# Graph attention on neighbour lists: weighing one step later in layer 1, and another staging place for its weight sums

## The chip, the cores and the metric

The kernel runs on one core of one Trainium2 chip, as one program. The metric is the time of an execution in device microseconds (us); where several executions were timed, their median is given. Besides the times there is a profiled execution, whose trace holds each instruction with its engine, its start and its length.

## The reference: what is computed

Two layers of graph attention are computed over N = 2708 tokens of width 512, with 8 heads of 64, in fp32. The adjacency matrix is symmetric, has a one on its diagonal and is otherwise about 0.3% full. Cut to what matters, one layer is:

```python
q = (h @ Wq + bq);  k = h @ Wk + bk;  v = h @ Wv + bv      # 8 heads of 64
scores = q @ k.T / sqrt(64), masked by adj                 # per head
cx = softmax(scores) @ v
h1 = layer_norm(h + cx @ Wo + bo)
out = layer_norm(h1 + relu(h1 @ W1 + b1) @ W2 + b2)        # W1: 512 -> 2048, W2 back
```

## The kernel before: tiles, stages, and what sets the order

**Tokens and neighbours.** The kernel sorts the tokens by their number of neighbours and cuts them into 22 tiles of 128 rows (the last has 20). A table gives each tile its number of neighbour slots, from 22 for the first tile down to 3. A slot is one gather on POOL's queue: 128 rows of keys and values, 128x1024 fp32, 512 KB, fetched from DRAM by a list of indices. A chunk is at most two slots, and lives in one `kv` buffer.

**One chunk of attention.** `weights` (L1154) forms the scores of a chunk on DVE: a product of keys and query (L1156), and a reduction to 8 heads a slot, `sc` (L1162). `weigh` (L1169) lets ACT take the exponentials `p` (L1175) and scale one of the two rows of values (L1182, eight instructions, one for each head), and DVE scale the other (L1188) and add both to a running sum `acc` (L1195). After a tile's last chunk come `sums` (L1199, DVE: L1203 to L1218) and `divided` (L1221, ACT, L1226, eight instructions), which leaves the tile's attention `cx`. The generator `attend` (L1895) makes these calls. In a step it emits the scores of one chunk, then `weigh` for the chunk of the step before, then `sums` for a tile that was weighed in full a step earlier, then `divided`.

**Dense work.** PE transposes `cx` into `cT` (`flip`, L1345: `tp` on PE at L1349, evicted by ACT at L1354), multiplies with Wo (`o`, L626), and runs the feed-forward. The first norm between them is spread over DVE (L1307, L1318, L1334), ACT (squares into `xb`, L1324, and `h<-h,rd`, L1340) and POOL (L1331, L1333). The feed-forward takes two tiles (a block) at a time, through 16 pieces f of 128 hidden columns: `pf` on PE, relu on ACT into `ft` (L1606, or L1778). There are 11 blocks k. From block 2 to block 9 it works by seven products of quarter matrices in place of eight ("by seven", products at L1756), which needs sums of quarters of W2, four for each of seven pairs j of its rows. These sums ("forms") are made on DVE and stored in DRAM, 512 KB a pair; `form_in` and `ask_forms` read them back in layer 1.

**The border of the layers.** While the last block of layer 0 runs, layer 1's matrices are loaded. Its keys and values go to DRAM (`keys_values`), its queries are projected by `query` (PE `q`, DVE `qs` at L1467) and stored (L1478, by SP's or ACT's queue). The transposed input `zT` of a tile is loaded again by SP, by `queries` (L1447, three buffers of tag `cT`, load at L1453) and `two` (L1440, load at L1444).

**Where the forms of layer 1 are staged.** `staged` takes three of the five `kv` buffers (six places of 512 KB), and `form_apart` forms pair j in place j modulo 6 and has ACT's queue store it. Pairs 0 and 1 come at f = 9 and 13 of layer 0's last block, 2 and 3 after its keys, 4, 5 and 6 at layer 1's start. The room of the matrices Wk and Wv (tags `wk` and `wv`, 1 MB each), which layer 1 no longer needs, serves as two more gather buffers from layer 1's first gather on, seven in all.

**Order.** Nothing reorders: each engine runs its instructions in the order in which the code emits them, and a queue issues its DMAs in that order. So an instruction that waits holds up all that stand behind it on its engine. Hand-written tables (`PACE7` and others) say how many steps of `attend` are emitted after each f.

Of the kernel before, what the change touches and what calls it, by code (L numbers as in the profile page):

```python
# [8 lines left out]
F32 = mybir.dt.float32  # L9
# [9 lines left out]
P = 128  # L19
DM = 512  # L20
# [3 lines left out]
NC = DM // P  # L24
# [13 lines left out]
SLOTS = 2  # L38
QB = 3
LAG = 3  # L40
KVB = 5
# [446 lines left out]
def by_edges(ctx: ExitStack, tc: tile.TileContext, x, xT, adj, layers, out, redo):  # L488
# [9 lines left out]
    nc = tc.nc  # L498
# [16 lines left out]
    wts = ctx.enter_context(tc.tile_pool(name="wts", bufs=1))  # L515
# [4 lines left out]
    stage = ctx.enter_context(ExitStack())  # L520
# [15 lines left out]
    at = None  # L536
# [6 lines left out]
    for _ in range(WARM):  # L543
# [16 lines left out]
    form_d = [  # L560
        dram.tile([NFC // 2 - 1, 3 + n, P, 2 * P], F32, name=f"form_d{n}") for n in range(NL)
    ]
# [576 lines left out]
    def chunks_of(g):  # L1139
        S = CAPS[g]  # L1140
        k = (S + SLOTS - 1) // SLOTS
        cuts = [-(-S * i // k) for i in range(k + 1)]
        return [(g, a, b - a) for a, b in zip(cuts, cuts[1:])]
# [87 lines left out]
    places = []  # L1231
    written = [[] for _ in range(NL)]

    def rows_of_keys(n):

        if n == NL - 1 and not places:
            places.extend([None] * KVB + ["wk", "wv"])
        tag = places[0] if places else None
        if places:
            places.append(places.pop(0))  # L1240
        if tag is None:
            return at.tile([P, SLOTS, 2 * DM], F32, tag="kv", name="kv", bufs=KVB)
        kv = wts.tile([P, NC, DM], F32, tag=tag, name="kv")
        return kv.rearrange("p c n -> p (c n)").rearrange("p (s n) -> p s n", s=SLOTS)
# [113 lines left out]
    class Layer:  # L1358
        def __init__(self, n, w):
            self.n, self.w, self.w1, self.w2, self.due = n, w, [], [], None  # L1360
            self.apart, self.other = True, False
            self.stores = nc.sync

# [304 lines left out]

        def staged(self):

            slots = []
            for _ in range(3):
                place = at.tile([P, SLOTS, 2 * DM], F32, tag="kv", name="forms", bufs=KVB)
                place = place.rearrange("p s (i w) -> p (s i) w", w=2 * P)
                slots += [place[:, i : i + 4] for i in (0, 4)]
            return slots

        def form_apart(self, j, slots):

            w, W = self.w2[j], 2 * P  # L1680
            b11, b12, b21, b22 = w[:, 0, :W], w[:, 0, W:], w[:, 1, :W], w[:, 1, W:]
            place = slots[j % len(slots)]
            t2, t3, t4, t1 = (place[:, i] for i in range(4))
            nc.vector.tensor_tensor(t3, b22, b12, ALU.subtract)
            nc.vector.tensor_tensor(t1, b12, b11, ALU.subtract)
            nc.vector.tensor_tensor(t2, b22, t1, ALU.subtract)
            nc.vector.tensor_tensor(t4, b21, t2, ALU.subtract)
            nc.scalar.dma_start(out=form_d[self.n][j].rearrange("i p w -> p i w"), in_=place)

        def form_in(self, j):  # L1690
            W = 2 * P
# [195 lines left out]
    now = Layer(0, layers[0])  # L1887
# [7 lines left out]
    def attend(n, got):  # L1895

        peak = small.tile([P, NT], F32, tag="peak", name="peak", bufs=1)
        nc.vector.memset(peak, 0.0)
        loaded = loads(n)
        steps = []  # L1900
        for g in order:
            cuts = chunks_of(g)
            steps += [(g, s0, c, i, i + 1 == len(cuts)) for i, (_, s0, c) in enumerate(cuts)]
            if g == order[1]:
                steps += [None] * 3
        steps += [None] * 3
        kv = next(loaded)
        yield 0.0
        q, later = asked(n, order[0]), None
        done = [None] * 3  # L1910
        for k, step in enumerate(steps):
            if step:
                g, s0, c, i, last = step
                if i == 0:
                    while q is None:
                        q = asked(n, g)
                        if q is None:
                            yield None
                    t, q = Tile(g, q), None
                if k > 0:  # L1920
                    kv = next(loaded)
                t.weights(kv, s0, c)
                if q is None and g != order[-1]:
                    q, later = later or asked(n, order[order.index(g) + 1]), None
                if g == order[-3] and i == 2:
                    later = asked(n, order[-1])
                done.append((t, kv, s0, c, last))
            else:
                done.append(None)
            t3, t2, t1 = done[-4:-1]  # L1930
            if t1:
                t1[0].weigh(*t1[1:4])
            if t2 and t2[-1]:
                t2[0].sums(peak)
            if t3 and t3[-1]:
                got[t3[0].g] = t3[0].divided()
            yield c / SLOTS if step else 0.2
        nc.vector.tensor_reduce(flags[:, 4 + n : 5 + n], peak, AX.X, ALU.max)
        nc.vector.tensor_scalar(
            flags[:, 4 + n : 5 + n], flags[:, 4 + n : 5 + n], SAFE, None, ALU.is_le  # L1940
        )
# [30 lines left out]

    got = {}
    ahead = attend(0, got)
    early = {}

# [39 lines left out]
    for n in range(NL):  # L2016
        last = n == NL - 1
        nxt = None if last else Layer(n + 1, layers[n + 1])
        if n > 0:
            streamed = now.queries(order[10:16])  # L2020
            got = {}
            ahead = attend(n, got)
            for j in (4, 5):
                now.query(*pool.pop(0))
                now.form_apart(j, staged)
            next(ahead)
            both = now.two(order[8:10])
            pool += [(g, both[:, i]) for i, g in enumerate(order[8:10])]
            next(streamed)
            now.stores = nc.scalar  # L2030
            now.form_apart(6, staged)
            while pool:
                if len(pool) < 5:
                    advance(0.65)
                now.query(*pool.pop(0))
            for i, _ in enumerate(streamed):
                if i == 1:
                    both = now.two(order[16:18])
                if i == 4:
                    now.stores = nc.sync  # L2040
                if len(got) < 2 or i < 3:
                    advance(0.65)
            until(blocks[0][0])
            early[n] = now.attended(blocks[0], got, None, True)
            next(early[n])
            now.query(order[16], both[:, 0])
            until(blocks[0][1])
            next(early[n])
            for _ in blocks[0]:
                next(early[n])  # L2050
            streamed = now.queries(order[18 : 2 * AHEAD])
            next(streamed)
            now.query(order[17], both[:, 1])
            advance(0.6)
            next(streamed)
            advance(0.6)
            *_, hs = early[n]
            early[n] = hs, now.turned(blocks[0], hs)
            asking = now.queries(blocks[AHEAD])
            next(asking)  # L2060
            finish(streamed)
            now.apart = False
            now.load_w2(NFC // 2 - 1)
        hs, hT = early[n]
        projecting = xbs = tail = None
        for k, block in enumerate(blocks):
# [14 lines left out]
            for f, zs in enumerate(working):  # L2081
# [31 lines left out]
                    now.load_w2(len(now.w2), nc.scalar)  # L2113
                if n > 0 and (k, f) == (0, 2):
                    now.load_second(1, temp)
                if n == 0 and k == FORMED[0] and f in FORMS:
                    now.form(FORMS.index(f))
                if n > 0 and k == FORMED[n] and f > 4 and f % 2:
# [27 lines left out]
                if not last and not more:  # L2146
                    if f % 2:
                        nxt.load_w1(f // 2)
                        if f > 2:
                            nxt.load_w2(f // 2 - 1)  # L2150
                    if f == 6:
                        nxt.load_first()
                        nxt.load_second(0, temp)
                        staged = nxt.staged()
                    if f in (9, 13):
                        nxt.form_apart(f // 4 - 2, staged)
                    if f == 13:
                        nxt.settle()
                    if f == 7:
                        finish(ahead)  # L2160
                        pool += nxt.preloaded(order[:8], temp)
# [5 lines left out]
        if not last:  # L2167
            nxt.wq = now.wq
            for _ in range(2):
                nxt.query(*pool.pop(0))  # L2170
                if len(pool) % 2:
                    next(behind)
            nxt.kept()
            for g in order[:2]:
                own[g] = asked(n + 1, g)
            finish(behind)
            behind = None
            for j in (2, 3):
                nxt.form_apart(j, staged)
            now = nxt  # L2180
    return again

# [54 lines left out]
```

## Time and profile before

| | |
|---|---|
| median of 3 runs | 1836.91 us (1832.55, 1836.91, 1836.97) |
| profiled execution | 1836.3 us, its span in the trace 1834.3 us |
| mean granted clock of PE in it | 0.994 |
| last keys of layer 0 issued to DRAM (POOL L1082) | 1075.03 us into the span |

PE is TensorE's matmuls, DVE is VectorE, ACT ScalarE, POOL GpSimd, SP SyncE; SPq, ACTq and so on are the sequencers that issue DMAs. In a row of the timeline, start and length come first, then engine, line, operation, output<-inputs and the number of instructions drawn together; in brackets stands the idle time ahead of it and what ended that. Among the DMA queues q0 carries POOL's transfers, q1 and q10 those of SP and ACT.

### The profile page before, as it was taken

The numbers are of one execution on the slowest core, as the hardware profiler recorded it, in microseconds if no ns is written. First come the engines' busy times: TensorE is split into PE (matmuls) and PEld (weight loads), VectorE is DVE, ScalarE is ACT, GpSimd is POOL, SyncE is SP. The second block draws the span as 40 slices with busy tenths as digits, with TensorE's granted clock in tenths as the row PEclk, the third lists the DMA queues.
The fourth block names the chain that finished last, engine by engine and source line by source line (L and its number), as shares of the span: only waits on it lengthen the run. The fifth ranks groups of instructions, "written<-read, shape, count | busy, mean of one in ns | idle before, by whom it ended". The sixth has DMA issues, their size and how long they took to land.

```text
span 1834.3 us, 24263 instructions
## 1 busy us (share of the span) xinstructions
PE 1794.1 (98%) x6931; PEld 1234.3 (67%) x6931; DVE 1483.3 (81%) x2667; ACT 1002.9 (55%) x3399; POOL 860.5 (47%) x827
## 2 busy tenths in 40 slices
PE   9999999999999999999999999999999999999997
PEld 4444456666777867778677543665787788788775
DVE  4987778988989889899885276988989988989952
ACT  4771435645556545564553112677666767667641
POOL 3333755534455544454430022645655655665512
PEclk9999999999999999999999999999999999999999
DMA  9997987756576675665652886957968776786721
GB/s 339 370 335 246 372 281 248 233 171 234 197 253 227 199 235 196 218 237 182 225 185 80 277 305 244 335 155 268 307 201 281 237 252 218 278 262 189 241 81 32
DMA packets 193928, 432.25 MB, mean 236 GB/s; under 512 B 21222, under 2 KB 91482, under 8 KB 193784
## 3 DMA queue, kind: packets, MB, share of 16 engines
q0 software_dynamic: 76560, 262.92, 42.9%
q1 hardware_dynamic: 103370, 142.42, 23.0%
q10 hardware_dynamic: 13854, 25.28, 3.7%
q8 instruction: 57, 0.93, 0.2%
q14 instruction: 87, 0.71, 0.1%
HBM read 362.63 MB, written 57.11 MB: 229 GB/s over the span
## 4 chain that ended last, share of the span: by engine, by line
PE 76%; DVE 12%; issue 5%; ACT 4%; DMA 2%; POOL 1%; DVEq 0%; POOLq 0%; ACTq 0%
PE pf L1767 18%; PE c L1756 8%; PE q L626 7%; PE k L626 7%; PE v L626 7%; PE o L626 7%; PE a L1756 6%; PE pf L1595 5%; PE a L1568 4%; DVE sc L1162 2%; DVE kv L1156 2%; PE tp L1349 2%; PE a L1787 1%; PE a L1791 1%; ACT kv L1182 1%
## 5 line engine op out<-in xcount | busy, mean ns | idle before, releaser
L1119 POOL DMA_INDIRECT kv<-kv_d,listed x420 | 538.2, 1282 | 295.0 <-DVE acc L1195 131.7
L1767 PE MATMUL pf<-hT,w 128*128 128x256 f32 x2048 | 465.6, 379 | 3.3 <-ACT ft L1778 3.3
L1767 PEld LDWEIGHTS pf<-hT,w 128*128 128x128 f32 x2048 | 387.4, 190 | 68.5 <-issue 12.0
L1182 ACT ACTIVATE kv<-kv,p 128x64 f32<-128x64 f32 x1232 | 311.0, 335 | 5.0
L1156 DVE TENSOR_TENSOR kv<-kv,q 128x1024 f32<-128x1024 f32 (+1 forms) x222 | 257.2, 1159 | 16.1 <-DMA q<-q_d,ident_i 10.9
L1162 DVE TENSOR_REDUCE sc<-kv 128x16 f32<-128x1024 f32 (+1 forms) x222 | 258.0, 1162 | 7.6
L1195 DVE TENSOR_TENSOR acc<-acc,kv 128x1024 f32<-128x1024 f32 (+2 forms) x178 | 205.6, 1155 | 51.6 <-ACT kv L1182 36.4
L1778 ACT ACTIVATE ft<-pf,b 128x256 f32<-128x256 f32 x192 | 88.8, 466 | 227.4 <-PE pf L1767 220.3
L1175 ACT ACTIVATE p<-sc,listed 128x8 f32<-128x8 f32 x420 | 103.5, 294 | 124.3 <-DVE sc L1162 96.0
L1281 POOL TENSOR_TENSOR rd<-va,mhalf 128x1 f32<-128x1 f32 (+1 forms) x48 | 43.8, 913 | 253.0 <-DVE va L1279 252.5
L626 PE MATMUL o<-wo,cT 128*128 128x512 f32 x336 | 152.8, 599 | 5.0 <-ACT ft L1606 3.6
L1595 PEld LDWEIGHTS pf<-hT,w 128*128 128x128 f32 x768 | 130.2, 190 | 39.5 <-issue 25.5
L1595 PE MATMUL pf<-hT,w 128*128 128x256 f32 (+1 forms) x768 | 155.1, 350 | 0.1
L1568 PE MATMUL a<-w,ft 128*128 128x512 f32 x288 | 135.1, 592 | 0.0
L1188 DVE TENSOR_TENSOR kv<-kv,p 128x512 f32<-128x512 f32 (+1 forms) x178 | 124.0, 697 | 5.9 <-ACT p L1175 5.7
L626 PEld LDWEIGHTS o<-wo,cT 128*128 128x128 f32 x336 | 64.0, 192 | 73.9 <-issue 61.1
L1331 POOL TENSOR_SCALAR va<-sq 128x1 f32<-128x1 f32 (+1 forms) x40 | 16.9, 424 | 200.3 <-ACT xb L1324 95.8
L751 DVE MAX8 tops<-code 128x8 f32<-128x247 f32 (+2 forms) x242 | 79.1, 400 | 29.3 <-ACT code L746 29.3
L1226 ACT ACTIVATE cx<-acc,su 128x64 f32<-128x64 f32 (+1 forms) x352 | 88.2, 333 | 11.1 <-DVE su L1218 8.6
L1182 ACT ACTIVATE acc<-kv,p 128x64 f32<-128x64 f32 (+1 forms) x352 | 88.9, 335 | 1.4
L746 ACT ACTIVATE code<-aj 128x1354 bf16<-128x1354 int32 (+1 forms) x44 | 74.0, 1724 | 25.9 <-POOL aj L740 21.8
L1756 PE MATMUL c<-w,forms 128*128 128x256 f32 x288 | 85.7, 379 | 0.0
(257 smaller groups left out, 2880.5 us busy)
## 6 DMA issues: line engine op xcount, KB each, us to landing
forms<-form_d SPq DMA_DIRECT2D x336, 128.0 KB
aj<-in_adj SPq DMA_DIRECT2D x42, 677.0 KB
kv_d<-kvs ACTq DMA_DIRECT2D x21, 512.0 KB
h<-ln_b POOLq DMA_DIRECT2D x41, 256.0 KB
xg<-in_xT SPq DMA_DIRECT2D x19, 512.0 KB
w<-in_W SPq DMA_DIRECT2D x16, 512.0 KB
kv<-kv_d,listed POOLq DMA_INDIRECT x420
zT_d<-zT SPq DMA_DIRECT2D x22, 256.0 KB
```

Of the source, the lines that this page charges most:

```text
L626: nc.tensor.matmul(o[:r], xs(c), wm[:, c, :], start=(c == 0), stop=(c == NC - 1))
L1119: return nc.gpsimd.indirect_dma_start(out=to, out_offset=None, in_=table[:, :], in_offset=bass.IndirectOffsetOnAxis(ap=s, axis=0), bounds_ ...
L1156: nc.vector.tensor_tensor(kv[:r, :c, :DM], kv[:r, :c, :DM], self.q[:r].unsqueeze(1).to_broadcast([r, c, DM]), ALU.mult,)
L1162: nc.vector.tensor_reduce(self.sc[:r, s0 : s0 + c, :], kv[:r, :c, :DM].rearrange("p s (h d) -> p s h d", d=DK), AX.X, ALU.add,)
L1175: nc.scalar.activation(p[:r, s, :], self.sc[:r, s, :], AF.Exp, bias=minus[:r, g, s : s + 1])
L1182: nc.scalar.activation(to[:, i, hd], kv[:r, i, DM + h * DK : DM + (h + 1) * DK], AF.Copy, scale=p[:r, s0 + i, h : h + 1],)
L1188: nc.vector.tensor_tensor(to[:, 0, :].rearrange("p (h d) -> p h d", d=DK), kv[:r, 0, DM:].rearrange("p (h d) -> p h d", d=DK), p[:r, s0, : ...
L1195: nc.vector.tensor_tensor(self.acc[:r, :c, :], self.acc[:r, :c, :], kv[:r, :c, DM:], ALU.add)
L1568: nc.tensor.matmul(a[:r, cols], fts[f][:, c0 : c0 + r], self.w2[f // 2][:, f % 2, cols], start=(f == 0), stop=(f == NFC - 1),)
L1595: nc.tensor.matmul(pf[:, :w], self.w1[f // 2][:, c, f % 2 * P : f % 2 * P + P], hT[:, c, :w], start=(c == 0), stop=(c == NC - 1),)
L1756: nc.tensor.matmul(to, left, right, start=start, stop=stop)
L1767: nc.tensor.matmul(pf[:, :W], self.w1[j][:, c, f % 2 * P : f % 2 * P + P], hT[:, c, :], start=(c == 0), stop=(c == NC - 1),)
```

## The change

The change has three parts.

1. In layer 1 `weigh` stands two steps behind the scores in place of one (`late = 1 + n`). `sums` and `divided` of a tile come at the start of the step after, ahead of that step's scores. Four empty steps in place of three let the tail run out. Layer 0 keeps its order.
2. The forms of layer 1 are staged elsewhere. Pairs 0, 1 and 2 are formed in two `kv` buffers in layer 0's last block (f = 9, 12, 15) and stored by POOL's queue. Pairs 3 and 4 are formed in the room of Wk after the last keys, pairs 5 and 6 in the room of Wv at layer 1's start.
3. These last four pairs are stored only in layer 1's first block, at f = 3 to 6, by SP's queue. The rooms of Wk and Wv become gather buffers behind that, at f = 7; until then gathers have five buffers.

```diff
     def rows_of_keys(n):
         if n == NL - 1 and not places:
-            places.extend([None] * KVB + ["wk", "wv"])
+            places.extend([None] * KVB)
...
         def staged(self):
-            slots = []
-            for _ in range(3):
-                place = at.tile([P, SLOTS, 2 * DM], F32, tag="kv", name="forms", bufs=KVB)
-                place = place.rearrange("p s (i w) -> p (s i) w", w=2 * P)
-                slots += [place[:, i : i + 4] for i in (0, 4)]
-            return slots
+            if not self.stages:
+                for _ in range(2):
+                    self.stages.append(
+                        at.tile([P, SLOTS, 2 * DM], F32, tag="kv", name="forms", bufs=KVB)
+                    )
+                return
+            for i, tag in enumerate(("wk", "wv")):
+                place = wts.tile([P, NC, DM], F32, tag=tag, name="forms")
+                self.stages.append(place.rearrange("p (s a) n -> p s (a n)", s=SLOTS))
+        def stage(self, j):
+            place = self.stages[j // 2 if j < 3 else (j + 1) // 2]
+            place = place.rearrange("p s (i w) -> p (s i) w", w=2 * P)
+            a = 4 * (j % 2 if j < 3 else (j + 1) % 2)
+            return place[:, a : a + 4]
-        def form_apart(self, j, slots):
+        def form_apart(self, j):
...
-            place = slots[j % len(slots)]
+            place = self.stage(j)
...
-            nc.scalar.dma_start(out=form_d[self.n][j].rearrange("i p w -> p i w"), in_=place)
+        def form_out(self, j, by):
+            to = form_d[self.n][j].rearrange("i p w -> p i w")
+            by.dma_start(out=to, in_=self.stage(j))
...
     def attend(n, got):
-        steps = []
+        steps, late = [], 1 + n
...
-                steps += [None] * 3
-        steps += [None] * 3
+                steps += [None] * (late + 2)
+        steps += [None] * (late + 2)
...
-        done = [None] * 3
+        done = [None] * 5
+        def ends():
+            t3, t2 = done[-3 - late], done[-2 - late]
+            if t2 and t2[-1]:
+                t2[0].sums(peak)
+            if t3 and t3[-1]:
+                got[t3[0].g] = t3[0].divided()
         for k, step in enumerate(steps):
+            if late > 1:
+                done.append(None)
+                ends()
+                done.pop()
...
-            t3, t2, t1 = done[-4:-1]
+            t1 = done[-1 - late]
             if t1:
                 t1[0].weigh(*t1[1:4])
-            if t2 and t2[-1]:
-                t2[0].sums(peak)
-            if t3 and t3[-1]:
-                got[t3[0].g] = t3[0].divided()
+            if late == 1:
+                ends()
...
-            for j in (4, 5):
+            for j in (5, 6):
                 now.query(*pool.pop(0))
-                now.form_apart(j, staged)
+                now.form_apart(j)
...
-            now.form_apart(6, staged)
...
+                if n > 0 and k == 0 and 2 < f < 7:
+                    now.form_out(f, nc.sync)
+                if n > 0 and (k, f) == (0, 7):
+                    places.extend(["wk", "wv"])
...
-                        staged = nxt.staged()
-                    if f in (9, 13):
-                        nxt.form_apart(f // 4 - 2, staged)
+                        nxt.staged()
+                    if f in (9, 12, 15):
+                        nxt.form_apart(f // 3 - 3)
+                        nxt.form_out(f // 3 - 3, nc.gpsimd)
...
-            for j in (2, 3):
-                nxt.form_apart(j, staged)
+            nxt.staged()
+            for j in (3, 4):
+                nxt.form_apart(j)
```

PE's order of instructions is the same in both kernels. The other engines' orders differ at many places; three follow.

ACT at the border, before: `kvs<-v` are the last values of layer 0, `form_d` the stores of forms, `q_d<-qs` the stores of queries, and `p` and `acc` the first weighing of layer 1.

```order
L1873 COPY kvs<-v 20x512
L1873 COPY kvs<-v 128x512
L1688 DMA form_d_118<-forms 128x4x256 x5
L1478 DMA q_d_114<-qs 128x512 x2
L1175 ACTIVATE p<-sc,listed 128x8 x2
L1182 ACTIVATE acc<-kv,p 128x64 x8
```

The same place on ACT in the changed kernel:

```order
L1886 COPY kvs<-v 20x512
L1886 COPY kvs<-v 128x512
L1479 DMA q_d_114<-qs 128x512 x3
L1175 ACTIVATE p<-sc,listed 128x8 x2
L1182 ACTIVATE acc<-kv,p 128x64 x8
```

The five stores of forms are gone from ACT's queue. POOL, at the same border in the changed kernel, has three of the seven stores, ahead of the last keys (`kv_d`) and the first gathers (`kv<-kv_d`):

```order
L1082 DMA kv_d_112<-kvs,ident_i 2708x1024 x2
L1701 DMA form_d_118<-forms 128x4x256 x3
L1281 TENSOR_TENSOR rd<-va,mhalf 20x1
L1281 TENSOR_TENSOR rd<-va,mhalf 128x1
L1869 MEMSET zT 128x512
L1082 DMA kv_d_112<-kvs,ident_i 2708x1024 x2
L1119 DMA kv<-kv_d_112,listed 128x1024 x18
```

The other four stand on SP's queue in layer 1's first block, among loads of layer-norm rows (`ln_b`) and of queries (`q<-q_d`):

```order
L581 DMA ln_b<-in_ln_b 128x512
L1701 DMA form_d_118<-forms 128x4x256 x2
L1116 DMA q<-q_d_114 128x512
L1701 DMA form_d_118<-forms 128x4x256 x2
L1479 DMA q_d_114<-qs 20x512
```

ACT at the end of block 4 of layer 1 (f = 12 to 15), before; the squares `xb,sq` and `h<-h,rd` are steps of the norm ahead of block 5, and `hT` evicts its transposes:

```order
L1324 ACTIVATE xb,sq<-h,nm 128x512
L1778 ACTIVATE ft<-pf,b_8175 128x256
L1175 ACTIVATE p<-sc,listed 128x8 x2
L1182 ACTIVATE kv<-kv,p 128x64 x8
L1226 ACTIVATE cx<-acc,su 128x64 x8
L1778 ACTIVATE ft<-pf,b_8175 128x256
L1340 ACTIVATE h<-h,rd 128x512 x2
L1778 ACTIVATE ft<-pf,b_8175 128x256
L1354 ACTIVATE hT<-tp,ln_b 128x128 x8
```

And in the changed kernel:

```order
L1324 ACTIVATE xb,sq<-h,nm 128x512
L1791 ACTIVATE ft<-pf,b_8175 128x256
L1175 ACTIVATE p<-sc,listed 128x8 x2
L1182 ACTIVATE acc<-kv,p 128x64 x8
L1791 ACTIVATE ft<-pf,b_8175 128x256
L1340 ACTIVATE h<-h,rd 128x512 x2
L1791 ACTIVATE ft<-pf,b_8175 128x256
L1354 ACTIVATE hT<-tp,ln_b 128x128 x8
L1226 ACTIVATE cx<-acc,su 128x64 x8
```

The eight `cx` moved from ahead of `h<-h,rd` to behind `hT`. At the end of block 3 eight `cx` stand ahead of `h<-h,rd` in both kernels.

DVE in the last block by seven (k = 9), before: a step's weighing is the pair L1188 and L1195, the sums for the seven products are L1733 to L1736, and L1203 begins the `sums` of the last tile:

```order
L1162 TENSOR_REDUCE sc<-kv 128x16
L1188 TENSOR_TENSOR kv<-kv,p 128x512
L1195 TENSOR_TENSOR acc<-acc,kv 128x1024
L1733 TENSOR_TENSOR forms<-ft 128x128
L1734 TENSOR_TENSOR ft<-ft 128x128
L1735 TENSOR_TENSOR forms<-forms,ft 128x128
L1736 TENSOR_TENSOR forms<-ft,forms 128x128
L1188 TENSOR_TENSOR kv<-kv,p 128x512
L1195 TENSOR_TENSOR acc<-acc,kv 128x1024
L1203 TENSOR_TENSOR acc<-acc 128x512
```

And in the changed kernel, from the same sums on:

```order
L1749 TENSOR_TENSOR forms<-ft,forms 128x128
L1188 TENSOR_TENSOR kv<-kv,p 128x512
L1195 TENSOR_TENSOR acc<-acc,kv 128x1024
L1188 TENSOR_TENSOR kv<-kv,p 128x512
L1195 TENSOR_TENSOR acc<-acc,kv 128x1024
L1746 TENSOR_TENSOR forms<-ft 128x128
L1747 TENSOR_TENSOR ft<-ft 128x128
L1748 TENSOR_TENSOR forms<-forms,ft 128x128
L1749 TENSOR_TENSOR forms<-ft,forms 128x128
L1203 TENSOR_TENSOR acc<-acc 128x512
```

One more weighing and one more set of sums for the products now stand between the last scores and the last tile's `sums`.

More of the change, by code (lines that the diff above doesn't have):

```diff
@@ L1360, in __init__ @@
             self.n, self.w, self.w1, self.w2, self.due = n, w, [], [], None
+            self.stages = []
             self.apart, self.other = True, False
```

## The prediction, made before the changed kernel ran

> **What bounds it now.** First the page: the busy times and their shares of the span.
>
> ```profile
> PE 1794.1 (98%) x6931; PEld 1234.3 (67%) x6931; DVE 1483.3 (81%) x2667; ACT 1002.9 (55%) x3399; POOL 860.5 (47%) x827
> ```
>
> PE is the bound, and the change leaves its instructions and their order alone. So a gain can come only from PE's idle time and from stretches at a lower clock. Second, PE's waits (us in total, times, longest):
>
> ```profile
> PE q L626 <- DMA zT<-zT_d: 4.5, 2, 3.6
> PE tp L1349 <- ACT h L1340: 4.2, 3, 2.4
> PE o L626 <- ACT ft L1606: 3.6, 1, 3.6
> PE pf L1767 <- ACT ft L1778: 3.3, 5, 1.1
> ```
>
> All four lie at the border or in layer 1 in the main. Third, the timeline of PE at the three large ones, and at two small ones:
>
> ```profile
> 1101.43 13.90 PE L626 MATMUL q<-wq,zT 128*128 128x512 f32 x32
> 1116.15 3.67 PE L626 MATMUL q<-wq,zT 128*128 128x512 f32 x8 [0.82 <-DMA zT<-zT_d]
> 1123.46 6.70 PE L626 MATMUL q<-wq,zT 128*128 128x512 f32 x8 [3.64 <-DMA zT<-zT_d]
> 1130.00 0.60 PE L1349 MATMUL tp<-ident,cx 128*128 128x128 f32 x4
> ...
> 1261.72 5.40 PE L626 MATMUL o<-wo,cT 128*128 128x512 f32 x8 [3.60 <-ACT ft L1606]
> 1401.74 1.99 PE L1767 MATMUL pf<-hT,w 128*128 128x256 f32 x8 [1.07 <-ACT ft L1778]
> 1466.99 1.73 PE L1349 MATMUL tp<-ident,h 128*128 128x128 f32 x8 [2.41 <-ACT h L1340]
> 1593.03 1.27 PE L1349 MATMUL tp<-ident,h 128*128 128x128 f32 x8 [1.41 <-ACT h L1340]
> ```
>
> Eight matmuls of q take 13.90 / 4 = 3.47 us, but 6.70 after the wait at the border, and eight of o 5.40. The windows say why; the third number from the end of a row, ahead of DMA share and GB/s, is the granted clock:
>
> ```profile
> 1125.00:1127.00 2.00, 2.00 (x3) 0.67 (x2) 1.93 (x6) 0.19 (x1) 0.00 (x0) 0.50 0.00 0
> 1260.00:1270.00 10.00, 8.28 (x23) 4.52 (x24) 9.43 (x15) 8.59 (x34) 2.02 (x2) 0.83 0.76 299
> 1465.00:1475.00 10.00, 8.01 (x29) 6.13 (x30) 7.92 (x12) 9.73 (x37) 7.72 (x7) 0.83 0.91 284
> ```
>
> After a long wait the clock stands at 0.50 for a while. A mean of 0.83 over 10 us is 3.4 us at half speed, some 1.7 us of work lost on top of the wait. So the three places cost: border, 1101.43 to 1130.00 is 28.6 us for six tiles worth 20.8, so 7.8 (4.5 of it waits); 1261, 3.6 + 1.7 = 5.3; 1467, 2.4 + 1.7 = 4.1. With the smaller waits (4.2 - 2.4 and 3.3, so 5.1 at most), all that the change can touch is about 22 us.
>
> By the Trainium skill (TensorE: Matmul & The Clock Gate, What's actually happening) the clock has two values, half and full, and falls after an idle window of about 3.4 us. The halves agree. The wait of 2.41 us at 1467 was followed by 3.4 us of half clock too, so here the measurement decides; counted by the page's figure, that place would be worth 2.4 in place of 4.1.
>
> **The border: stores taken away.** The late loads are the fifth and sixth zT. The DMA engines are the cause:
>
> ```profile
> DMA packets 5603, 10.56 MB, mean 341 GB/s; under 512 B 402, under 2 KB 2962, under 8 KB 5602
> ...
> q0 software_dynamic: 424, 1.54, 67.9%
> q10 hardware_dynamic: 212, 0.40, 17.3%
> q1 hardware_dynamic: 213, 0.39, 16.8%
> ```
>
> The first row is 1074 to 1105, the queues are 1110 to 1116 (packets, MB, share): the engines are full, mostly with POOL's gathers (q0). The issues around it:
>
> ```profile
> 1074.22 11.08 ACTq L1688 DMA_DIRECT2D form_d<-forms  x5
> ...
> 1095.72 0.99 POOL L1119 DMA_INDIRECT kv<-kv_d,listed  x1 [7.37 <-DVE kv L1156]
> ...
> 1105.06 3.75 SPq L1453 DMA_DIRECT2D zT<-zT_d  x2
> 1111.92 0.32 SPq L1453 DMA_DIRECT2D zT<-zT_d  x1
> ```
>
> The sixth zT, asked at 1111.92, is read at 1123.46, 11.5 us for 256 KB. To be in time it would have to be there at 1116.15 - 0.82 + 3.47 = 1118.8, 4.7 us sooner. Removed from these 31 us are the five stores, 5 x 0.52 = 2.6 MB: 7.7 us of DMA at 341 GB/s. Two of them freed the `kv` buffers that held POOL up to 1095.72; after that it issued twelve gathers back to back, 6.3 MB, into the window in which the zT were asked. With five gather buffers in place of seven, 2 MB of these come later still. Against that, three stores (1.6 MB) move to POOL's queue ahead of the last keys: formed at f = 9 to 15, some 20 us sooner, so two are gone before; only the third (1.5 us at 341) may push the keys. I take it as hidden by the projections that run on PE then. Net 2.6 MB + up to 2 MB less, 7.7 to 13 us against the 4.7 needed: both zT in time. PE then runs on to the transpose of block 0's second `cx`:
>
> ```profile
> 1126.81 0.35 ACT L1226 ACTIVATE cx<-acc,su 128x64 f32<-128x64 f32 x1 [2.57 <-DVE su L1218]
> ```
>
> This `cx` was ready at 1128.8, and PE would want it near 1125.7 with nothing lost. It comes sooner with no gather late, and later by the step that `weigh` stands back, for which DVE has room (it waits 1.54 us for a gather at 1103, quoted below). Estimate: 1 us of wait remains. Bounds: nothing to 7.8 gained; I take -7.0.
>
> **Weighing two steps back.** At 1261 PE waits for `ft`, and ACT was held up ahead of it, by scores just made:
>
> ```profile
> 1258.52 0.49 ACT L1175 ACTIVATE p<-sc,listed 128x8 f32<-128x8 f32 x2 [1.41 <-DVE sc L1162]
> ...
> 1260.96 0.45 ACT L1606 ACTIVATE ft<-pf,b 128x256 f32<-128x256 f32 x1
> ...
> 1251.69 1.22 DVE L1156 TENSOR_TENSOR kv<-kv,q 128x1024 f32<-128x1024 f32 x1
> 1256.01 1.22 DVE L1156 TENSOR_TENSOR kv<-kv,q 128x1024 f32<-128x1024 f32 x1
> ```
>
> A chunk is 4.32 us of DVE. Two steps back, `p` asks for scores 4.3 us older, so the wait of 1.41 and the lateness behind it go: -5.3 (bounds 0 and -5.3). What DVE waits for ACT goes the same way:
>
> ```profile
> DVE acc L1195 <- ACT kv L1182: 15.7, 18, 1.6
> 1127.00:1757.00 630.00, 620.08 (x2565) 472.02 (x2563) 558.62 (x902) 428.16 (x1545) 356.55 (x323) 0.99 0.74 242
> ```
>
> (Waits, then the window, both of layer 1: DVE is busy 558.6 of 630 us, 89%.) But DVE is the next bound. PE comes 12 us sooner to blocks 2 and 3 and DVE has its chunks still to do, so part comes back: at block 3's end eight `cx` (2.0 us of ACT) still stand ahead of `h<-h,rd`, where PE lost 1.07 at 1401. I take +1 in block 2 and +2.5 in block 3, between nothing and the whole 5.3.
>
> At 1467 the reason is on ACT in plain sight:
>
> ```profile
> 1463.97 2.00 ACT L1226 ACTIVATE cx<-acc,su 128x64 f32<-128x64 f32 x8
> 1466.23 1.32 ACT L1340 ACTIVATE h<-h,rd 128x512 f32<-128x512 f32 x2
> ```
>
> Without these eight `cx` (they move behind `hT`), `h<-h,rd` comes 2.0 sooner; of the wait of 2.41 0.4 to 0.5 remains and the half clock goes: -3.4. For the other small waits I take -1.5 of 5.
>
> The last block pays. There the last tile's `cx` is what PE waits for next:
>
> ```profile
> 1752.26 0.28 DVE L1733 TENSOR_TENSOR forms<-ft 128x128 f32<-128x128 f32 x1
> 1753.39 0.68 DVE L1188 TENSOR_TENSOR kv<-kv,p 128x512 f32<-128x512 f32 x1
> 1755.44 0.69 DVE L1203 TENSOR_TENSOR acc<-acc 128x512 f32<-128x512 f32 x1
> ...
> 1757.03 2.02 ACT L1226 ACTIVATE cx<-acc,su 128x64 f32<-128x64 f32 x8 [0.98 <-DVE su L1218]
> 1758.05 1.38 PE L1349 MATMUL tp<-ident,cx 128*128 128x128 f32 x4
> ```
>
> One set of sums (1752.26 to 1753.39, 1.1) and one weighing (2.0) come ahead of L1203 in addition, and the transposes follow `cx` at once: +3.0, less where DVE is ahead by then (bounds 0 and 3.1, and with half clock behind it 4.8).
>
> The four stores on SP in layer 1's first block cost nothing by themselves: 2.1 MB, 6 us of DMA that the gathers share, while PE there never stopped.
>
> ```profile
> 1150.00:1160.00 10.00, 10.00 (x40) 7.41 (x39) 8.32 (x11) 8.15 (x33) 8.48 (x8) 1.00 1.01 387
> ```
>
> Their cover is DVE's slack there, 17%. SP's loads of queries stand behind them, asked a tile ahead.
>
> Sum: -7.0 - 5.3 + 3.5 - 3.4 - 1.5 + 3.0 = -10.7, from 1836.3 to 1825.6. That execution is 0.6 under the median of 1836.9, so 1826.
>
> **Rivals.** *All of it goes:* DVE's 15.7 us of waits give it the room, nothing comes back and the last block pays nothing: -7.8 - 5.3 - 4.1 - 4 = -21, 1815.5. For it: 11% of DVE idle. Against: the order in the last block. Chance 0.15.
>
> *The zT stay late:* between 1110 and 1116 three queues share, 68 : 17 : 17, so that SP's queue gets its 17% share as long as POOL's has gathers, whatever was stored before. Then 256 KB still take about as long as now, the border gives 1 to 3 in place of 7: 1831 to 1833. The Trainium skill has this (DMA: Bandwidth & Descriptors, Queues, rings and completion order): each engine takes turns among the queues, a packet each; the 424, 212 and 213 packets agree in so far as the two hardware queues have equal counts. Against: the backlog behind the sharing is what shrinks. Chance 0.12.
>
> *DVE takes it back:* what layer 1 gains in one block it waits for in the next, as DVE is 89% busy; only the border's 7 less the last block's 3 remain: 1832.5. Chance 0.09.
>
> *Slower, five buffers starve DVE:* at the border a gather released at 1095.72 was read at
>
> ```profile
> 1103.84 1.23 DVE L1156 TENSOR_TENSOR kv<-kv,q 128x1024 f32<-128x1024 f32 x1 [1.54 <-DMA kv<-kv_d,listed]
> ```
>
> 8.1 us later. With five buffers, each now held a step longer, the cover is two chunks, 2 x 4.32 = 8.6. It decides from 8.6 on: with the stores of forms in the same stretch a landing of 10.5 would cost 1.9 for each of some 14 chunks, 27 us of DVE against 17% slack over 80 us, 14; the rest, 13, shows on PE in blocks 0 and 1, less the border's 7 and 3 more: 1840. Chance 0.10.
>
> **Numbers.** The forecast has 0.54, its own range 1821 to 1831. Low 1816 leaves out half of the first rival, high 1838 most of the last: together under 2 in 10. A measurement of this kernel tells 0.3%, 5.5 us: faster is forecast and first rival, 0.69 + 0.01; same is the two at 1832 to 1833, 0.21; slower the last, most of it, 0.09.
>
> **What would show it.** Right: in PE's waits the row q <- zT is gone, no 0.50 at 1125; no o <- ft; no 2.4 of tp <- h, a wait of tp for `cx` near 1755 instead. DVE's wait for L1182 well under 15.7. Wrong: DVE kv <- DMA rows between 1130 and 1210; POOL gathers that wait for L1188 or L1195 there; tp <- h or pf <- ft rows of the old sum at other blocks.

## The result: slower by 0.56%, and the profile after

The changed kernel takes 1844.61 us in the median of 7 runs (1841.11 to 1847.77), the kernel before 1833.24 of 7 (1831.03 to 1836.97). The ratio is 1.0056, with a 95% interval of 1.0041 to 1.0072: slower by about 11 us, outside the forecast range and on the other side of zero. The profiled execution took 1847.77 us (span 1845.7).

PE's busy time and its waits, from the page and the view of waits of the changed kernel (us in total, times, longest):

```profile
PE 1800.1 (98%) x6931; PEld 1238.0 (67%) x6931; DVE 1484.4 (80%) x2667; ACT 1000.9 (54%) x3399; POOL 844.1 (46%) x830
```

```profile
PE pf L1780 <- ACT ft L1791: 8.7, 5, 4.2
PE o L626 <- ACT cT L1354: 7.6, 4, 5.2
PE tp L1349 <- ACT h L1340: 4.0, 3, 2.3
...
PE tp L1349 <- ACT cx L1226: 2.6, 2, 2.5
```

The row of q waiting for zT is gone (4.5 before), and so is o waiting for ft (3.6). In their place stand waits for `cT`, for `ft` in the blocks by seven, and for `cx`. The timeline of PE shows where. (The two o of a block are multiplied inside the feed-forward of the block before it: those of block 1 begin at 1196, inside block 0, and those of block 2 at 1263 and 1272, inside block 1.)

```profile
1105.28 20.80 PE L626 MATMUL q<-wq,zT 128*128 128x512 f32 x48
...
1196.39 6.28 PE L626 MATMUL o<-wo,cT 128*128 128x512 f32 x7 [5.17 <-ACT cT L1354]
...
1263.21 3.60 PE L626 MATMUL o<-wo,cT 128*128 128x512 f32 x8
1272.30 3.27 PE L626 MATMUL o<-wo,cT 128*128 128x512 f32 x7 [1.61 <-ACT cT L1354]
...
1409.55 1.27 PE L1349 MATMUL tp<-ident,h 128*128 128x128 f32 x8 [2.28 <-ACT h L1340]
...
1721.78 2.50 PE L1780 MATMUL pf<-hT,w 128*128 128x256 f32 x5 [4.17 <-ACT ft L1791]
...
1769.37 1.91 PE L1349 MATMUL tp<-ident,cx 128*128 128x128 f32 x4 [2.48 <-ACT cx L1226]
```

The first row is the border: all six tiles of queries run through in 20.8 us, without a wait. At the first o of block 1 the kernel before had

```profile
1194.14 3.70 PE L626 MATMUL o<-wo,cT 128*128 128x512 f32 x8 [0.40 <-ACT cT L1354]
```

PE's instructions stand in one order in both kernels, so the start of each can be set against its like. Over the border the changed kernel gains 6.6 us against the kernel before, and at the first o of block 2 (1263) another 5.6. It loses 7.8 at the first o of block 1 (1196, a wait of 5.17 where 0.40 was, and half clock), 1.9 at 1272, 6.3 in blocks 2 and 3, 4.6 in block 8 (1721) and 5.4 in the last block by seven (1769), and gains 3.7 from block 4 to block 7. From the border to PE's last matmul layer 1 is 16.7 us longer; behind that, while the last rows go out, it gains 2.7. (Ahead of layer 0's last block, where the two kernels have the same order, the changed one's execution is already 3.8 us behind. That is a spread between executions: the kernel below with cheaper empty steps has the changed kernel's order up to the border as well, and its execution comes there 5.6 us sooner.)

DVE's waits in layer 1, in the changed kernel:

```profile
DVE acc L1195 <- ACT kv L1182: 22.9, 23, 1.6
DVE kv L1188 <- ACT p L1175: 9.1, 9, 2.0
...
DVE kv L1156 <- DMA kv<-kv_d,listed: 3.3, 2, 2.2
```

DVE waits more for ACT than before (L1195 15.7, L1188 2.5), though its scores are a chunk older. It waits little for gathers, 3.3 us in all, but 2.24 of them stand ahead of the wait at 1196:

```profile
1165.17 1.23 DVE L1156 TENSOR_TENSOR kv<-kv,q 128x1024 f32<-128x1024 f32 x1 [2.24 <-DMA kv<-kv_d,listed]
```

### The profile page after: what moved, and what is told of

It reads as the page before. It is cut to its first block, busy times and chain, and to the rows that moved or that the text cites. A ratio compares the mean times of both kernels' runs of the same rounds, so it can differ in the third digit from the quotient of the medians.

```text
span 1845.7 us, 24269 instructions
## 1 busy us (share of the span) xinstructions
PE 1800.1 (98%) x6931; PEld 1238.0 (67%) x6931; DVE 1484.4 (80%) x2667; ACT 1000.9 (54%) x3399; POOL 844.1 (46%) x830
## 5 line engine op out<-in xcount | busy, mean ns | idle before, releaser
L1119 POOL DMA_INDIRECT kv<-kv_d,listed x420 | 524.2, 1248 | 370.5 <-DVE acc L1195 174.6
L1195 DVE TENSOR_TENSOR acc<-acc,kv 128x1024 f32<-128x1024 f32 (+2 forms) x178 | 205.6, 1155 | 60.1 <-ACT kv L1182 43.4
L1188 DVE TENSOR_TENSOR kv<-kv,p 128x512 f32<-128x512 f32 (+1 forms) x178 | 123.7, 695 | 13.7 <-ACT p L1175 12.3
L1769 PE MATMUL a<-w,forms 128*128 128x256 f32 x288 | 85.7, 379 | 0.0
```

The lines of the kernel that those rows point to most:

```text
L1119: return nc.gpsimd.indirect_dma_start(out=to, out_offset=None, in_=table[:, :], in_offset=bass.IndirectOffsetOnAxis(ap=s, axis=0), bounds_ ...
L1188: nc.vector.tensor_tensor(to[:, 0, :].rearrange("p (h d) -> p h d", d=DK), kv[:r, 0, DM:].rearrange("p (h d) -> p h d", d=DK), p[:r, s0, : ...
L1195: nc.vector.tensor_tensor(self.acc[:r, :c, :], self.acc[:r, :c, :], kv[:r, :c, DM:], ALU.add)
L1769: nc.tensor.matmul(to, left, right, start=start, stop=stop)
```

## The experiments

The kernels were timed in three sets, each beside the kernel before (the third set on another chip). The median of the latter moved between 1831.5 and 1835.4 from set to set, so ratios are given against the runs of the same set.

**First set: the parts apart.** The staging alone, weighing one step behind:

```diff
-        steps, late = [], 1 + n
+        steps, late = [], 1
```

> The staging of the forms as in the change, weighing one step behind in layer 1 as before. Theory 1 (the loss lies in the weighing two steps behind; the staging is good): the border keeps its gain of 6.6 us, the wait of 3.6 us for ft at block 1 and the 2.4 us at block 4 stay; 1826 to 1829 against 1833 before, PE's wait o <- cT at block 1 under 1 us or back by part of the gain. Theory 2 (five buffers and stores moved into block 0 cost more than they bring): 1836 to 1842, with DVE waits for gathers (kv <- DMA) over 10 us in layer 1.

Measured: 1826.64 us against 1835.4, ratio 0.9953 (0.9941 to 0.9966). PE's waits of this kernel from the border on:

```profile
PE tp L1349 <- ACT h L1340: 3.9, 3, 2.1
PE o L626 <- ACT ft L1607: 3.6, 1, 3.6
PE q L626 <- DMA zT<-zT_d: 2.3, 2, 1.3
...
PE o L626 <- ACT cT L1354: 0.3, 1, 0.3
```

Layer 1 is as before, the border is cheaper (2.3 of waits for zT without half clock behind them, not nothing), and behind the border DVE waits for no gather. Theory 2 falls.

The weighing two steps behind alone, with the staging as before (the loop of `attend` from the changed kernel, its four empty steps with it, in the kernel before):

> Weighing two steps behind with the sums and cx at the next step's start, the forms staged as before. Theory 1: the border still costs its 7.8 us, and layer 1 loses: PE comes to block 0 6.6 us later, so that the new wait of 5.2 us for cT there is nearly gone, the others (ft 4.2 us in block 8, cx 2.5 us in the last block, half clock behind them) stay: 1839 to 1845. DVE's waits for ACT (L1195 and L1188) at 25 us or more, as in the change (32), against 18 before. Theory 2: 1826 to 1830, since only the lag's gains are left.

Measured: 1844.99 us, 1.0059 (1.0046 to 1.0072). Theory 1's upper end: without the better border it is as slow as the whole change, and its waits in block 8 (4.2) and for the last `cx` (2.8) are those of the changed kernel. The wait at the first o of block 1, expected to be nearly gone with PE later there, is 3.0:

```profile
1195.99 3.70 PE L626 MATMUL o<-wo,cT 128*128 128x512 f32 x8 [3.00 <-ACT cT L1354]
```

DVE's two waits for ACT were 32.4 us. For gathers, with seven buffers, it did not wait behind the border.

The whole change, with `cx` at the end of a step in place of the next one's start:

```diff
-            if late > 1:
-                done.append(None)
-                ends()
-                done.pop()
+            if late > 1:
+                add_up(1)                 # sums of the tile weighed in the step before
...
-            if late == 1:
-                ends()
+            if late == 1:
+                add_up(0)
+            divide(late - 1)              # cx of the tile whose sums this step made
```

> The change, with the division cx taken from the next step's start to the end of the step in which the sums are made (behind that step's weighing, and ahead of the dense work that is emitted between two steps). Theory 1 in the form that cx comes too late on ACT, behind ft that wait for PE: PE's waits for cx and cT (10.2 us in layer 1) fall by half or more, 1836 to 1841. If DVE's pace alone sets layer 1: no change, 1843 to 1846.

Measured: 1838.35 us, 1.0015 (1.0006 to 1.0025). So some 6 us (1844.6 to 1838.4) come back by the place of `cx` in the order alone. But PE's waits for `cT` and `cx` fell only from 10.2 to 9.4 us; those for `ft` fell, from 7.1 to 3.7 with the 1.3 that the view gives to issue. The time was as expected, the place was not.

The whole change with three empty steps behind the first block's tiles:

```diff
             if g == order[1]:
-                steps += [None] * (late + 2)
+                steps += [None] * 3
```

> The change, with three empty steps in place of four behind the first block's tiles, as before. If the extra empty step is what makes the scores of block 1's tiles fall behind a query that PE makes late (DVE waited 3.6 us for q at 1149 there): PE's wait for cT at 1196 (5.2 us and 3.4 at half clock) falls to 2 or less, 1837 to 1840. If DVE was late for other reasons: 1843 to 1846.

Measured: 1831.21 us (1828.49 to 1836.15), 0.998 (0.9969 to 0.9991), below both readings. One empty step, which adds no instruction, is worth 13.4 us in the medians; in the profiled executions 10.9 of it lie between the border's first query and PE's last matmul. But again not where expected: the wait for `cT` at block 1 stayed, and those in block 8 and for the last `cx` were gone.

```profile
PE o L626 <- ACT cT L1354: 6.4, 2, 4.7
PE tp L1349 <- ACT h L1340: 5.4, 4, 1.4
PE q L626 <- DMA zT<-zT_d: 2.6, 1, 2.6
PE pf L1780 <- ACT ft L1791: 0.8, 1, 0.8
```

**Second set: why an empty step costs.** `attend` is paid by the piece: after each f its steps are emitted while a budget lasts, a chunk of two slots costs 1 and an empty step 0.2. One empty step more puts later steps 0.2 later against PE's pieces. (Steps that are emitted because PE's next work needs a tile's `cx` are not paid, so that equal prices in sum need not give an equal order.)

```diff
-            yield c / SLOTS if step else 0.2
+            yield c / SLOTS if step else 0.6 / (late + 2)
```

> The change with its four empty steps, each paid at 0.15 of a step in place of 0.2, so that the four cost the order's budget what three did. If the loss of 13 us between four and three empty steps comes from the budget (all later steps of attention are emitted 0.2 of a step later against PE's pieces f): 1830 to 1834. If it comes from the empty step itself (block 0's second tile ends a step later): 1841 to 1846.

Measured: 1835.05 us (1829.32 to 1841.44), 1.0002 (0.9987 to 1.0016). 9.6 of the 13.4 us come back; the median lies a little above the range that was expected, and the runs lie 12 us apart. So the price of empty steps alone, without an instruction more or less, moves the time by some 10 us. But the order that it gives is not that of three steps, and PE's waits are others:

```profile
PE pf L1780 <- ACT ft L1791: 6.6, 3, 4.4
PE o L626 <- ACT cT L1354: 3.8, 2, 2.8
...
PE tp L1349 <- ACT cx L1226: 1.5, 1, 1.5
```

The wait in block 8 (4.4) is there, as with four steps at the full price; the gain lies between the first o of block 1 and block 4. That the shift by 0.2 makes the difference between three and four steps, place for place, is thus not shown.

The same empty step without the lag (in the staging alone, four in place of three, and this in both layers):

> Staging alone (weighing one step behind), with four empty steps at 0.2 in place of three. If the place of the steps against the pieces f is what costs, with or without the lag: 1833 to 1842 against 1826.6 with three. If an empty step more hurts only together with the lag: 1825 to 1829.

Measured: 1833.84 us, 0.9992 (0.9981 to 1.0002), so 7.2 us more than the staging alone, whose ratio was 0.9953 (0.9941 to 0.9966). Not all of it is layer 1's. The edit lengthens layer 0's order too, and of the 8.1 us between the two profiled executions 4.4 lie ahead of the border, 2.7 of them as waits that the staging alone doesn't have:

```profile
276.92 1.99 PE L1596 MATMUL pf<-hT,w 128*128 128x256 f32 x8 [1.75 <-ACT ft L1607]
292.32 1.99 PE L1596 MATMUL pf<-hT,w 128*128 128x256 f32 x8 [0.93 <-ACT ft L1607]
```

From the border on the fourth step costs 3.7 us, between the two readings. In layer 1 the two orders differ at few places, and the trace shows one chain whole. DVE with three empty steps, and then with four:

```profile
1141.38 0.69 DVE L1468 SCALAR_TENSOR_TENSOR qs<-q,bq 128x512 f32<-128x512 f32 x1 [0.36 <-PE q L626]
1141.99 1.22 DVE L1156 TENSOR_TENSOR kv<-kv,q 128x1024 f32<-128x1024 f32 x1
...
1145.69 0.69 DVE L1468 SCALAR_TENSOR_TENSOR qs<-q,bq 128x512 f32<-128x512 f32 x1 [0.64 <-PE q L626]
```

```profile
1144.89 0.69 DVE L1468 SCALAR_TENSOR_TENSOR qs<-q,bq 128x512 f32<-128x512 f32 x1 [0.36 <-PE q L626]
1149.20 0.69 DVE L1468 SCALAR_TENSOR_TENSOR qs<-q,bq 128x512 f32<-128x512 f32 x1 [3.62 <-PE q L626]
1149.81 1.22 DVE L1156 TENSOR_TENSOR kv<-kv,q 128x1024 f32<-128x1024 f32 x1
```

With three, a chunk's scores stand between two `qs`; with four, the second `qs` has come ahead of them, and DVE waits for PE to finish that query, 3.62 us, with the scores behind it. 44 us later PE, which has not waited since, finds the first o of block 1 short of its `cT`; the first row is with three empty steps, the second with four:

```profile
1187.19 3.70 PE L626 MATMUL o<-wo,cT 128*128 128x512 f32 x8 [0.32 <-ACT cT L1354]
```

```profile
1193.54 4.97 PE L626 MATMUL o<-wo,cT 128*128 128x512 f32 x7 [3.15 <-ACT cT L1354]
```

The changed kernel has the same pair of `qs`, with the same 3.62 us:

```profile
1145.57 0.69 DVE L1468 SCALAR_TENSOR_TENSOR qs<-q,bq 128x512 f32<-128x512 f32 x1 [0.36 <-PE q L626]
1149.88 0.69 DVE L1468 SCALAR_TENSOR_TENSOR qs<-q,bq 128x512 f32<-128x512 f32 x1 [3.62 <-PE q L626]
```

On ACT the lateness arrives as a wait for DVE's sums `su`, and the eviction `cT`, whose transposes PE had finished at 1187.8, stands behind it:

```profile
1188.48 2.02 ACT L1226 ACTIVATE cx<-acc,su 128x64 f32<-128x64 f32 x8 [4.06 <-DVE su L1218]
...
1195.98 1.11 ACT L1354 ACTIVATE cT<-tp,bv 128x128 f32<-128x128 f32 x4
```

But the lag with three empty steps has the pair too (3.62, at 1150.70), and so its wait at block 1 stayed. From the second `qs` to the first o of block 1 it takes 44.3 us with the fourth step and no lag, and 44.2 with the lag and the staging as before, but 46.5 in the changed kernel, whose DVE waits 2.24 for a gather in between, and 45.9 with three empty steps, where that wait is 1.5. So this wait for a gather, which needs the lag and the new staging together, makes the rest of the 5.17.

Both repairs together, three empty steps and `cx` behind the weighing:

> The change with three empty steps and cx behind the weighing of the step in which its sums are made. If both repairs add up (13.4 and 6.3 us): 1824 to 1826. If they mend the same waits: 1829 to 1834.

Measured: 1833.94 us, 0.999 (0.9981 to 1.0). They don't add up; both together are no better than three empty steps alone, since this order has waits of its own again (3.0 for `cT`, 2.5 for the last `cx`).

The lag only where it had gained, not where layer 1 begins. `attend` is rewritten so that each chunk carries its own lag; the line that decides is shown. It gives the lag from the seventh tile on, the first of block 3, so blocks 0 to 2 have one step and the rest two:

```diff
+                late = 2 if n and order.index(g) >= SWITCH else 1     # SWITCH = 6
```

> Staging as in the change, three empty steps, weighing one step behind for the first six tiles of layer 1 and two behind from the seventh tile on, so that blocks 0 and 1 have the one and the rest the other. If the lag only hurts where five buffers and a late DVE stand at block 1: no new wait at 1196, the wait of 3.6 for ft at block 1 goes: 1819 to 1824. If the lag hurts everywhere or not by its place: 1828 to 1834.

Measured: 1830.52 us, 0.9973 (0.9962 to 0.9984). In its profiled execution (1828.3 us) the waits for `cT` at 1196 and for `ft` at 1263 are both gone, and those of block 8 (ft, 4.4) and of the last `cx` (2.5) are back: half of each reading.

**Third set: the lag in the middle, and what the border gained by.** From the last kernel, the lag is also ended again:

```diff
+                late = 2 if n and SWITCH <= order.index(g) < BACK else 1     # 6 and 14
```

> Staging as in the change, three empty steps, weighing two steps behind for the 7th to the 14th tile of layer 1 alone (blocks 3 to 6), one behind ahead of and after them. If the lag's cost sits at the end (ft in block 8, the last cx) and its gain at block 1 (wait of 3.6 for ft and half clock): 1818 to 1822. If the steps' places against the pieces f shift by the lag in any case, so that waits come back elsewhere: 1825 to 1831.

Measured: 1818.61 us (1817.82 to 1820.29) against 1831.45, ratio 0.9925 (0.9907 to 0.9943). This is the fastest of all, and beats both kernels. Against the staging alone (0.9953, 0.9941 to 0.9966, in another set) the lag in the middle is worth some 5 us; the two intervals just touch. PE's waits in its layer 1, none over 1.4 us:

```profile
PE tp L1350 <- ACT h L1341: 3.2, 3, 1.4
PE pf L1781 <- ACT ft L1792: 2.0, 4, 0.9
PE q L627 <- DMA zT<-zT_d: 0.8, 2, 0.4
```

With the lag for four tiles alone (`BACK = 10`):

> The same with the two steps for the 7th to the 10th tile alone. First reading: 1820 to 1823 (the wait at block 1 gone, those of 2 us at blocks 4 and 6 kept). Second: 1825 to 1831.

Measured: 1821.43 us, 0.9938 (0.9919 to 0.9956), as the first reading had it. DVE still waited 23.1 us for ACT's scaled values (there L1183) in the kernel of 1818.61, as much as in the changed kernel (22.9): their sum is not what costs.

The prediction put the border's gain down to fewer stores and to later gathers at once. The kernel before, with five gather buffers up to f = 7:

```diff
-            places.extend([None] * KVB + ["wk", "wv"])
+            places.extend([None] * KVB)
...
+                if n > 0 and (k, f) == (0, 7):
+                    places.extend(["wk", "wv"])
```

> The kernel before, with the rooms of Wk and Wv added to the gather buffers only at f = 7 of layer 1's first block, as in the change; forms staged and stored as before. If the border gains because gathers come later: PE's loss there falls from 7.8 to 2 or less, 1827 to 1830. If because the stores are gone: 1833 to 1837, zT late as before.

Measured: 1832.15 us, 1.0001 (0.9989 to 1.0012); q waits 4.2 us for zT, as before. And the kernel before without the stores of pairs 2 to 6 (layer 1 then reads layer 0's forms for them, so that it loads as much and doesn't compute what the reference does):

> The kernel before without the stores of layer 1's forms of pairs 2 to 6 (layer 0's forms are read in their place, so the numbers differ and the traffic does not); seven gather buffers. If the stores' 2.6 MB make the zT late: loss at the border from 7.8 to 2 or less, 1827 to 1830. If the burst of gathers does: 1832 to 1836.

Measured: 1827.53 us, 0.997 (0.9959 to 0.9981). Its six tiles of queries run through as in the changed kernel:

```profile
1101.57 21.05 PE L626 MATMUL q<-wq,zT 128*128 128x512 f32 x48
```

So it is the stores. Whether by their bytes or by the `kv` buffers that they hold is not separated: without them POOL issues its gathers without the pause of 7.37 us, up to 1095.72, that it has before. Five buffers alone neither help nor harm.

## Why the prediction was wrong, point by point

**Where the loss comes from, in medians.** Staging -8.8 us (1835.4 to 1826.6); the lag with three empty steps +4.6 (to 1831.2); the fourth empty step +13.4 (to 1844.6). The first three were timed in one set, the last in another, in which the kernel before was 2 us faster; by the ratios the four are 1, 0.9953, 0.998 and 1.0056, which gives nearly the same steps. In the profiled executions, from the border's first query to PE's last matmul, they take 718.7, 712.8, 718.1 and 729.0 us: steps of -5.9, +5.4 and +10.9.

**The border: right.** -7.0 was forecast, and 6.6 came. The reason was half right: the stores are shown by the kernel without them; the later gathers, half of the argued relief, do nothing alone.

**The wait for ft inside block 1: right.** -5.3 forecast, -5.6 measured, and in every kernel that has the lag there PE waits at most 1.05 us at that o, and not for `ft`. The reading of it, that `p` stood behind scores just made and held up `ft`, fits that.

**The end of block 4: right.** -3.4 forecast, -3.9 measured; the wait of 2.41 for `h<-h,rd` fell to 0.12.

**The step that failed: DVE's room where layer 1 begins.** The prediction saw that a tile's `cx` comes "later by the step that `weigh` stands back, for which DVE has room", left 1 us of wait for it at the border, and added nothing for the tiles behind. At the border this held (PE waits 0.68 us for `cT` in block 0). At the first o of block 1 it did not: 7.8 us that stand nowhere in the sum, a wait of 5.17 with half clock behind it. In place of room the traces show DVE idle for 3.62 us at a query, with a chunk's scores slipped behind it, and then for 2.24 at a gather. The first is brought by the empty step without the lag (a wait of 3.15 at PE) and by the lag without the empty step (4.70, with 1.5 for a gather in it). The second stands in the kernels with the lag and the new staging there, and not where one of the two is missing. It is one of the prediction's own signs of being wrong: "DVE kv <- DMA rows between 1130 and 1210".

**The empty step: no term.** The change names a fourth empty step, and the sum has nothing for it. It cost 13.4 us in the medians with the lag. It is a unit of the budget that sets the emission, so steps behind it move against PE's pieces, and on an engine that runs in order a step that slips behind one dense instruction inherits the wait of that instruction. Between three empty steps and four, with the lag, the difference lies mainly in block 8 and in the last block by seven, not at block 1.

**Block 8: not seen.** +4.6, and nothing in the sum. The change's order was shown at three places on ACT and DVE; this is a fourth. There the rows of ACT and DVE in the changed kernel are

```profile
1709.71 0.72 ACT L1324 ACTIVATE xb<-h,nm 128x512 f32<-128x512 f32 x1 [5.58 <-DVE nm L1318]
...
1710.43 2.00 ACT L1226 ACTIVATE cx<-acc,su 20x64 f32<-20x64 f32 x8
...
1718.12 0.72 ACT L1324 ACTIVATE xb<-h,nm 128x512 f32<-128x512 f32 x1 [2.90 <-DVE nm L1318]
```

```profile
1714.90 1.23 DVE L1195 TENSOR_TENSOR acc<-acc,kv 128x1024 f32<-128x1024 f32 x1 [1.55 <-ACT kv L1182]
```

and ACT in the kernel before has

```profile
1703.46 0.72 ACT L1324 ACTIVATE xb<-h,nm 128x512 f32<-128x512 f32 x1 [2.07 <-DVE zsum L1307]
...
1709.97 0.72 ACT L1324 ACTIVATE xb<-h,nm 128x512 f32<-128x512 f32 x1 [2.90 <-DVE nm L1318]
```

Eight `cx` of the short tile fell between the norm's two `xb`: p and kv come 2 us later, DVE waits for them with the norm's sum behind it, ACT gets that sum later, with `ft` behind it, and PE waits 4.17. The two `xb` are 8.4 us apart where they were 6.5; that is half of the wait. The other half is there already at the first `xb`, which comes 2.1 us later against PE. Four kernels have the `cx` at this place (the changed one, the lag alone, the four cheap steps, the lag from the seventh tile on), and PE waits 4.2 to 4.4 us in each. With three empty steps and with `cx` at the end of a step they stand ahead of both `xb`, and there is no wait.

**The last block by seven: right, and too small.** +3.0 was taken, with 4.8 as a bound where half clock follows; 5.4 came: a wait of 2.48 and half clock behind it.

**Blocks 2 and 3 (+3.5 forecast, +6.3 measured), blocks 4 to 7 (-4.9 forecast, -3.7).** What comes back was undersized: at the end of block 3 the wait for `h` alone is 2.28, with half clock behind it. The other small waits, -1.5 in the sum, gave nothing. Together with 1.9 at the second o of block 2, the terms that were put at nothing (block 1, block 2 and block 8) are 14.3 of the 20.8 us between the forecast of -10.7 and the 10.1 that these places add up to.

**The rivals.** That five buffers starve DVE was right in kind and far too large: 27 us of waits for gathers were named, 3.3 came, of which 2.24 count at block 1; five buffers without the lag are at a ratio of 1.0001. That the zT stay late because queues share is out too. "DVE takes it back" was nearest in kind, but at 1832.5 it stopped at giving back; the runs show that more than the gain can go. A shift of steps by the budget had no chance in the list. What is left open: why the four steps at the price of three give waits at other places than three steps, and stay 3.8 us above them in the medians (in the profiled executions, from the border to PE's last matmul, the two are alike: 718.3 and 718.1).

## What to carry to other kernels

Where one loop's steps are doled out between another loop's pieces, a step that adds no instruction is not free: ask which in-order instruction each moved step now stands behind, at every piece and not at three, since one slip shows up as a wait far away, 44 us later here. Check also that an edit for one stage leaves the others alone: an empty step meant for layer 1 also moved layer 0 here. A deeper software pipeline is worth its lag where a wait for just-made data is seen (inside block 1), and cost here where the pipeline starts and drains; deep in the middle alone, with three empty steps, it turned 1844.6 into 1818.6 us. When two parts of a change lie apart, time them apart before judging either: here one was worth 8.8 us and the other hid it.

## What the runs showed of the hardware that was not expected

The price of a wait at PE is not fixed by its length. After a wait of 2.28 us the clock was at half for some 3.4 us of the next 7 (row one, third number from the end), while a wait of 3.00 us in the kernel with the lag alone left it at 1.00 (row two, windows of 7 us behind the wait).

```profile
1409.00:1416.00 7.00, 6.45 (x24) 5.10 (x25) 4.78 (x9) 6.93 (x26) 6.08 (x6) 0.76 0.91 310
```

```profile
1196.00:1203.00 7.00, 7.00 (x24) 4.11 (x25) 6.83 (x8) 4.61 (x18) 2.72 (x2) 1.00 0.98 360
```

So the 1.7 us that the prediction added to each long wait came behind some and not behind others. The Trainium skill (TensorE: Matmul & The Clock Gate, What's actually happening) says that the window over which activity is judged is free-running and isn't reset when a kernel starts. If it doesn't begin with a wait either, which is inferred here, a shorter wait can be the dearer one; the two rows agree with that and don't show it.
